# Scan operands with three PSUM banks instead of a rotation through four, decays in one piece in every scan, and a norm's first pieces issued inside a tick

## The chip, the cores and the metric

The kernel runs on one core of a Trainium2 chip, as one launch. A core has five engines with a queue of instructions each, which they work off in order: TensorE (PE in the profile, its weight loads PEld), VectorE (DVE), ScalarE (ACT), GpSimd (POOL) and SyncE (SP, which only starts DMAs here). Semaphores make one engine wait for another. The matmul results lie in PSUM, 8 banks of 128 x 512 float32. The metric is the device time of one execution in microseconds (us), as the median of several runs.

## The reference

Four blocks are added to an image x of shape (4, 128, 64, 64), one after the other; each first normalises its input over groups of channels (`_gn`). The third one, a state space scan, fills most of the time:

```python
x = x + attention(_gn(x))              # 1x1 q, k, v; softmax over the 4096 pixels
x = x + conv5x5(_gn(x))                # weights built from tables
t = einsum('oc,bchw->bohw', Wx, _gn(x)) + bx        # third block, per image
xF, xR = t[:, :64], flip(t[:, 64:])    # 64 channels forwards, 64 backwards
  xc = silu(conv1d(u, conv_w, 4 taps) + conv_b)
  delta = softplus(xc @ Wd + bd)
  Bm, Cm = xc @ WB, xc @ WC            # 64 states
  h[t] = exp(delta * A) * h[t-1] + (delta * xc) * Bm     # for 64 x 64 rows, 4096 steps
  y = sum_n h * Cm + D * xc
x = x + Wp @ concat(yF, flip(yR)) + bp
x = x + conv3x3(_gn(x)) + main_b       # offsets are computed in the reference and not used
```

## The kernel before, in words

All is float32. `program` (L1667) builds the work; the order of instructions on every engine is that in which the Python code issues them.

**The scan.** `scan_core` (L1426) goes through 1024 ticks, 256 an image: 4 chunks of 1024 pixels, 2 directions, 16 groups of 4 states, 2 groups of 32 channels; a tick handles 128 rows (32 channels x 4 states) of 1024 pixels. Its steps, each issued some ticks from the others in the loop over `i` (L1628):
- `drive(i + 2)`, L1535, GpSimd: `db = dx * br`. Both are read back from DRAM with replication, `dx` (delta * xc) and `de` (delta) by `steps`, `br` and `cr` (rows of Bm and Cm) by `row`. There are three buffers of `db`.
- `decay(i + 1)`, L1528, ScalarE: `da = exp(a * de)` into PSUM.
- `recur(i)`, L1545, VectorE: the scan instruction. It reads `da` and `db`, and takes `before`, the last column of the chunk ahead. Either its result goes to `hc` and GpSimd multiplies it with `cr` a tick later (`weigh`, L1566), or it goes back to `da` and VectorE multiplies (L1548) into `hc`. `to_pool` (L1448) chooses.
- `collect(i - 3)`, L1584, TensorE: sums `hc` over the states, into the bank "y".

**What lies beside it.** `images()` is a generator with all other work: attention, 5x5 convolution (`conv_pairs`) and scan operands of the next image, then the ends and 3x3 convolutions of earlier images. After each half tick the loop adds `pace / 2` of credit (`PACES`, L47: 2.60 in the first image's scan, 2.57 in the second and third, 1.55 in the last), and pulls pieces of that work until their announced costs use it up. A cost is what the generator yields: 0.86 for a product, 1.7 for a `HOP`, 0.7 for a `SLOT`.

**The operands.** `scan_prep` (L1237) settles the norm's sums (`settle`, L359: a few small VectorE steps, a small matmul, then two small GpSimd steps, which wait for the next tick by `next_tick`), and normalises the image in 8 pieces (L424, ScalarE). Ahead of six of them it waits while "wide" is there. `scan_operands` (L1262) then writes a list of slots. A chunk of 512 pixels, `i`, has slots from 5i on: taps (L1284, TensorE: four taps, forwards and backwards, into the bank `pt`), `halves` (L1299 and L1306, ScalarE: half of the sum, and tanh), `silu` (L1310, VectorE), three products (L1319) into the bank `pz` (for delta) and twice into "a" (the rows, which L1325 copies out), `softplus` (L1333, L1334), `exp` (L1362, L1368), `digits` (L1339, L1340, VectorE). `logs` (L1375) come in blocks of several chunks, since they load another table on ScalarE; after them `join` (L1347), the store of `dd`, `drives` (L1352, GpSimd) and its store `dxd`. Each slot yields 0.7. For the first image the operands of the first two chunks are made before tick 0; for the others all of them lie in the last ticks of the scan of the image before.

**The banks.** "s", "z", "a" and "y" are there always. The other four have two uses. Outside the operand stages they hold two decays of 1024 columns (pool "wide"). In a stage `widen` (L1805) closes this pool between two ticks and opens another one: "s2", one bank for the operands, and three of 512 columns for decays in halves; a scan is then two scans of 512. `pt` and `pz` go through "s", "z" and "s2" in turn. The two kinds of tick are told apart in `decay` and `recur` by `"wide" in pools`.

Of the kernel before, what the change touches and what calls it, by code (L numbers as in the profile page):

```python
# [32 lines left out]
P = 128  # L33
# [12 lines left out]
PRODUCT, VALUES, HOP, SLOT, AHEAD, EARLY = 0.86, 0.9, 1.7, 0.7, 4, 8  # L46
PACES = 2.60, 2.57, 2.57, 1.55  # L47
# [6 lines left out]
def conv_preact_kernel(  # L54
# [275 lines left out]
    class Sums:  # L330
# [28 lines left out]
        def settle(self, name, wait=False):  # L359
# [14 lines left out]
            if wait:  # L374
                yield from next_tick()
            nc.gpsimd.tensor_tensor(rs, var, mhalf, ALU.pow)
            nc.gpsimd.tensor_tensor(nb, minus, rs, ALU.mult)
            return rs, nb

# [72 lines left out]
    def attention_start(b, xn):  # L452
# [19 lines left out]
        def keys(i):  # L472

            tag = "saz"[i % 3] if b == 0 else "s" if i < 3 or i % 2 == 0 else "s2" if "s2" in pools else "z"
            pvs[i] = bank(tag, f"pv_{b}_{i}").rearrange("p (t c) -> p t c", c=C)
            for t in range(TPM):
                nc.tensor.matmul(
                    pvs[i][:, t, :], xn[:, bass.ts(i * TPM + t, P)], wv, start=True, stop=True
                )
# [547 lines left out]
    def conv_pairs(b, xs, tag, st, st2, lean):  # L1027
# [207 lines left out]
        ready.update({(b, "convolved"), "narrow"})  # L1235
# [4 lines left out]
    def scan_prep(b, xs, st, mats4):  # L1240
# [4 lines left out]
        gn = yield from st.settle(f"s{b}", True)  # L1245
        xn = pools["big"].tile([P, VSIZE], F32, tag="V", name=f"xn2_{b}")
        nc.gpsimd.memset(xn[:, :pad], 0.0)
        nc.gpsimd.memset(xn[:, pad + L : 2 * pad + L], 0.0)

        def piece(*chunks):  # L1250
            for i in chunks:
                cut = slice(i * MM, (i + 1) * MM)
                normalise(xn[:, pad + cut.start : pad + cut.stop], xs[:, cut], gn)
# [3 lines left out]
        piece(0)  # L1257
        piece(NM - 1)
        while "wide" in pools:
            yield HOP  # L1260
        return scan_operands(b, xn, mats4, piece)

    def scan_operands(b, xn, mats4, piece):
# [10 lines left out]
        def taps(i, *ks):  # L1274
            if ks[0] == 0:
                pts[i] = bank(ring["pt", i], f"pt_{b}_{i}")
# [65 lines left out]
        def join(c):  # L1342
            for i in range(c * CH // MM, (c + 1) * CH // MM):
                cut = bass.ts(i, MM)

                eng = nc.vector if b > 0 and NM // 2 <= i < NM - 1 else nc.gpsimd
# [8 lines left out]
        def delta_product(i):  # L1355
            pzs[i] = product(i, 0, ring["pz", i])
# [13 lines left out]
        def logs(i, j):  # L1370
            for n in range(i, j):
                to = us[n]
                if b > 0 and j == NM and n - i < 3:
                    to = bank(("a", "z", "s2")[n - i], f"ln_{b}_{n}")
# [5 lines left out]
        order = sorted([(EVERY * i, "pt", i) for i in range(NM)] + [(EVERY * i + 8, "pz", i) for i in range(NM)])  # L1380
        ring = {(what, i): ("s", "z", "s2")[n % 3] for n, (_, what, i) in enumerate(order)}
        ring["pz", NM - 1] = "z"
# [5 lines left out]
        for i in range(NM):  # L1388
# [3 lines left out]
            at(t + 4, halves, i)  # L1392
            at(t + 5, silu, i)
            at(t + 8, delta_product, i)
            at(t + 9, row_product, i, 1)
            at(t + 10, softplus, i)
            at(t + 11, row, i, 1)
            at(t + 12, exp, i)
            at(t + 12, row_product, i, 2)
            at(t + 13, digits, i)  # L1400
            at(t + 13, row, i, 2)
# [3 lines left out]
        for i, j in zip(cuts, cuts[1:]):  # L1405
            t = EVERY * (j - 1) + 15
            at(t, logs, i, j)
            for n, c in enumerate(range(i // PER, j // PER)):
                at(t + 1 + n, join, c)
                at(t + 3 + n, drives, c)  # L1410
                at(t + 4 + n, ready.add, (b, "operands", c))
# [5 lines left out]
        at(EVERY * (NM - 1) + 13, ready.add, "drives")  # L1417
        ready.add("operands")
        for t in range(max(slots) + 1):
            for f, args in slots.get(t, ()):  # L1420
                f(*args)
            yield SLOT
        ready.discard("operands")
        ready.discard("drives")
        ready.discard("narrow")
# [5 lines left out]
    def scan_core(mats4, ynds, before, widen, result):  # L1431
# [16 lines left out]
        def to_pool(i):  # L1448


            if i not in pooled:
                n = i % 5
                pooled[i] = (
                    i % 3 == 2 if "wide" in pools
                    else n == 1 if "drives" in ready
                    else n % 2 == 0 if "operands" in ready else n % 2 == 1
# [60 lines left out]
        def decay(i, h):  # L1517
            b, c, d, q, g = ticks[i]
            if h == 0:
                das[i] = []  # L1520
            elif "wide" in pools:
                return

            wide = "wide" in pools
            size = CH if wide else MM
            da = in_turn(*(("wide", "da", 2) if wide else ("s2", "half", 3)), [P, size], f"da_{i}_{h}")
            das[i].append(da)
            nc.scalar.activation(  # L1528
                da, rep["de", b, c, d, g][:, bass.ts(h, size)], AF.Exp, scale=a_neg[:, at(i)]
# [7 lines left out]
        def recur(i):  # L1537
# [3 lines left out]
            size = CH // len(das[i])  # L1541
            for n, da in enumerate(das.pop(i)):
                cut = bass.ts(n, size)
                h = hc[:, cut] if to_pool(i) else da
                nc.vector.tensor_tensor_scan(h, da, db[:, cut], before, ALU.mult, ALU.add)  # L1545
                before = h[:, size - 1 : size]
                if not to_pool(i):
                    nc.vector.tensor_tensor(  # L1548
                        hc[:, cut], h, rows["c", b, c, d, q][:, cut], ALU.mult
                    )  # L1550
            hcs[i], hold[i] = hc, before
# [78 lines left out]
        for i in range(-AHEAD, n + 4):  # L1630
# [5 lines left out]
            late = i + 1 < n and i >= 0 and widen()  # L1636
            if not late:
                do(decay, i + 1, 0)
            do(recur, i)
            if late:  # L1640
                do(keep, i)
                late()
                do(decay, i + 1, 0)
# [6 lines left out]
            do(decay, i + 1, 1)  # L1650
# [19 lines left out]
    def program(safe):  # L1670
# [3 lines left out]
        ready.add("narrow")  # L1674
# [120 lines left out]
        with ExitStack() as es, tc.manual_schedule():  # L1795
# [3 lines left out]
            banks = es.enter_context(ExitStack())  # L1799
# [155 lines left out]
```

## Time and profile before

| what | value |
|---|---|
| median of 3 runs | 4184.01 us (4183.44 to 4185.94) |
| the profiled execution, its own time | 4187.43 us |
| its span, first to last instruction | 4184.1 us |
| busy share: TensorE, VectorE, ScalarE, GpSimd | 88%, 84%, 56%, 84% |
| decays of 1024 columns, of 512 | 963, 122 |
| mean of such a decay | 1117 ns, 697 ns |
| before the first scan | 685.3 us |
| ticks | 685.3 to 4118.4 us |

The profile has a page of totals for the execution and, from the same trace, other views: busy time of each engine in given stretches, the instructions in order of time, groups of equal instructions, and sums of waits. In a line of instructions, `out<-in` are tiles by name, then come shapes; in brackets stands how long the engine was idle before it, and what released it. An instruction's duration overlaps the start of the next one by up to 0.1 us, so costs in a row are better taken from one start to the next.

### The profile page before, as it was taken

How to read it: one execution, taken by the hardware profiler on the slowest of the kernel's cores; microseconds unless marked ns; L12 is line 12 of the kernel's file. 1: busy time of each engine (PE TensorE's matmuls, PEld its weight loads, DVE VectorE, ACT ScalarE, POOL GpSimd, SP SyncE). 2: the span in 40 equal slices, each digit the busy share in tenths (PEclk: the TensorE clock that was granted, in tenths of full speed). 3: DMA queues.
4: the chain of work that ended last, by engine and by line, in shares of the span. 5: the costliest groups of instructions: out<-in, count | busy, mean ns of one | idle time of the engine just before them, and what ended most of it. 6: DMA issues, size and time to landing. Idle time of an engine off the chain costs nothing. (4 is left out here: it accounts for less than half of the span.)

```text
span 4184.1 us, 49830 instructions
## 1 busy us (share of the span) xinstructions
PE 3687.0 (88%) x17668; PEld 2140.8 (51%) x17668; DVE 3514.0 (84%) x2441; ACT 2325.1 (56%) x3900; POOL 3525.7 (84%) x1688
## 2 busy tenths in 40 slices
PE   8999997999999979999999889999998576675856
PEld 4444443778875327887763368787733121221212
DVE  3842215999999979999999899999998899999996
ACT  3344306667665476766664676666645654545442
POOL 2433315999999979999999799999998899999995
PEclk9999998999999989999999999999999788797877
DMA  1020006555555666555555575555655756666661
GB/s 66 31 104 26 3 11 239 196 191 191 195 190 190 192 240 222 197 192 194 192 190 193 203 253 195 191 197 185 204 179 197 258 199 230 205 213 224 211 234 61
DMA packets 223728, 740.99 MB, mean 177 GB/s; under 512 B 29662, under 2 KB 30942, under 8 KB 223212
## 3 DMA queue, kind: packets, MB, share of 16 engines
q1 hardware_dynamic: 221548, 736.99, 52.0%
q8 instruction: 140, 2.29, 0.2%
q14 instruction: 120, 0.98, 0.1%
q10 hardware_dynamic: 1920, 0.73, 0.1%
HBM read 662.14 MB, written 75.47 MB: 176 GB/s over the span
## 5 line engine op out<-in xcount | busy, mean ns | idle before, releaser
L1535 POOL TENSOR_TENSOR db<-dx,br 128x1024 f32<-128x1024 f32 x1024 | 2398.5, 2367 | 119.4 <-DVE hc L1545 44.6
L1528 ACT ACTIVATE da<-de,a_neg 128x1024 f32<-128x1024 f32 (+1 forms) x1085 | 1160.3, 1070 | 375.2 <-DVE hc L1548 272.6
L1545 DVE TENSOR_TENSOR_SCAN da<-da,last,db 128x1024 f32<-128x1024 f32 (+1 forms) x500 | 1152.8, 2306 | 21.7 <-ACT last L1561 10.6
L1548 DVE TENSOR_TENSOR hc<-da,cr 128x1024 f32<-128x1024 f32 (+1 forms) x698 | 824.7, 1182 | 61.8 <-issue 1.3
L1566 POOL TENSOR_TENSOR hc<-hc,cr 128x1024 f32<-128x1024 f32 x354 | 837.4, 2366 | 6.8 <-ACT last L1561 3.6
L1584 PE MATMUL y<-hc,sel 128*32 128x512 f32 x4096 | 601.3, 649 | 270.2 <-POOL hc L1566 206.9
L748 PEld LDWEIGHTS acc<-v,exchange 128*128 128x128 f32 x6144 | 799.7, 191 | 48.3 <-issue 10.6
L727 PE MATMUL sc<-r,x 128*128 128x256 f32 x3072 | 803.0, 386 | 21.2 <-ACT exchange L740 16.2
L748 PE MATMUL acc<-v,exchange 128*128 128x129 f32 x6144 | 803.3, 275 | 1.5 <-ACT exchange L740 1.5
L727 PEld LDWEIGHTS sc<-r,x 128*128 128x128 f32 x3072 | 527.9, 191 | 188.5 <-ACT exchange L740 41.2
L1545 DVE TENSOR_TENSOR_SCAN hc<-da,last,db 128x1024 f32<-128x1024 f32 (+1 forms) x268 | 597.3, 2229 | 7.0 <-ACT last L1561 3.6
L740 ACT ACTIVATE exchange<-sc 128x512 f32<-128x512 f32 x768 | 441.8, 588 | 171.9 <-PE sc L727 164.6
L1584 PEld LDWEIGHTS y<-hc,sel 128*32 128x32 f32 x4096 | 113.6, 113 | 620.6 <-POOL hc L1566 303.4
L1545 DVE TENSOR_TENSOR_SCAN da<-da,db 128x1024 f32<-128x1024 f32 (+1 forms) x170 | 376.6, 2215 | 14.9 <-ACT da L1528 10.5
L1561 ACT COPY last<-da 128x1 f32<-128x1 f32 x511 | 80.4, 157 | 542.9 <-DVE hc L1548 541.9
L549 POOL TENSOR_TENSOR sidep<-sidep,exchange 128x512 f32<-128x512 f32 x120 | 165.0, 1375 | 254.3 <-ACT exchange L531 251.9
L531 ACT ACTIVATE exchange<-sc 128x512 f32<-128x512 f32 x256 | 152.6, 596 | 254.5 <-PE sc L530 246.5
L549 DVE TENSOR_TENSOR sided<-sided,exchange 128x512 f32<-128x512 f32 x120 | 98.5, 821 | 214.7 <-ACT exchange L531 213.6
L537 PE MATMUL acc<-exchange,v 128*128 128x512 f32 x512 | 261.9, 594 | 0.9
L530 PE MATMUL sc<-r,x 128*128 128x512 f32 x512 | 262.1, 594 | 0.6 <-ACT r L513 0.6
L893 PE MATMUL pcm<-xpm,cs 128*128 128x512 f32 x432 | 213.0, 643 | 10.3 <-ACT xpm L424 10.3
L1545 DVE TENSOR_TENSOR_SCAN hc<-da,db 128x1024 f32<-128x1024 f32 (+1 forms) x86 | 190.7, 2218 | 7.6 <-ACT da L1528 5.1
(295 smaller groups left out, 3048.6 us busy)
## 6 DMA issues: line engine op xcount, KB each, us to landing
br<-bm SPq DMA_DIRECT2D x512, 512.0 KB, 4.0
cr<-cm SPq DMA_DIRECT2D x512, 512.0 KB, 4.6
dx<-dxd SPq DMA_DIRECT2D x64, 512.0 KB, 5.3
de<-dd SPq DMA_DIRECT2D x64, 512.0 KB, 6.3
xs<-in_x_dram SPq DMA_DIRECT2D x16, 512.0 KB, 6.0
xsd<-xs SPq DMA_DIRECT2D x16, 512.0 KB, 5.2
xcd<-xc SPq DMA_DIRECT2D x16, 512.0 KB, 2.6
bm<-bs SPq DMA_DIRECT2D x32, 256.0 KB, 5.4
```

Of the source, the lines that this page charges most:

```text
L530: nc.tensor.matmul(sc, xn[:, bass.ts(j, P)], rq[blk], start=True, stop=True)
L537: nc.tensor.matmul(acc[blk], v[:, j, :C], ring[:, u % NRING, :], start=j == 0, stop=j == NJT - 1)
L549: eng.tensor_tensor(s, s, ring[:, u % NRING, :], ALU.add)
L727: nc.tensor.matmul(sc[:, bass.ts(n, HM)], xn[:, bass.ts(2 * k + n, P)], rq[blk][:, cut], start=True, stop=True,)
L740: nc.scalar.activation(pt, sc, AF.Exp)
L748: nc.tensor.matmul(acc[part][:, bass.ts(t, CV)], ring[:, u % NRING, n * HM + t * P : n * HM + (t + 1) * P], v[:, 2 * k + n, :], start=(k, ...
L1528: nc.scalar.activation(da, rep["de", b, c, d, g][:, bass.ts(h, size)], AF.Exp, scale=a_neg[:, at(i)])
L1535: nc.gpsimd.tensor_tensor(dbs[i], rep["dx", b, c, d, g], rows["b", b, c, d, q], ALU.mult)
L1545: nc.vector.tensor_tensor_scan(h, da, db[:, cut], before, ALU.mult, ALU.add)
L1548: nc.vector.tensor_tensor(hc[:, cut], h, rows["c", b, c, d, q][:, cut], ALU.mult)
L1566: nc.gpsimd.tensor_tensor(hcs[i], hcs[i], rows["c", b, c, d, q], ALU.mult)
L1584: nc.tensor.matmul(y[r : r + SG, :], sel, hcs[first + gg][:, bass.ts(h, MM)], start=False, stop=q == NQ - 1, tile_position=(0, r), skip_gr ...
```

## The change

- The pool "wide" is opened once, ahead of the ticks, and stays. `widen`, "s2" in the scans, and the halves of decays and scans are gone; each decay has 1024 columns, and each scan is one instruction.
- The operands use three banks in a fixed way: `pt` "s", `pz` "z", the rows "a". The last logs of an image go to two banks, not three, and one `join` less is on VectorE. `keys` of the next image take "s" while operands are made.
- The slots of a chunk are moved: halves from 4 to 3, silu from 5 to 4, the delta product from 8 to 6, softplus from 10 to 7, and so on; digits from 13 to 10. Logs stand at 11 after the last chunk's first slot and not at 15. A slot yields `STEP` = 0.9 as long as chunks are in work; the slots behind that wait for the next tick. `PACES` are 2.66, 2.60, 2.60 and 1.57.
- `settle` leaves its GpSimd steps and the norm's pieces 0 and 7 to a hook. The loop over ticks runs it just ahead of the next decay.
- `to_pool`: while operands are made, ticks with i mod 5 of 2 or 4 are weighed on GpSimd (before: 0, 2, 4), while the last products are made those of 1 (as before), otherwise each third (before, in the stretches with "s2" and no operands: 1 and 3 of 5).

```diff
-PRODUCT, VALUES, HOP, SLOT, AHEAD, EARLY = 0.86, 0.9, 1.7, 0.7, 4, 8
-PACES = 2.60, 2.57, 2.57, 1.55
+PRODUCT, VALUES, HOP, SLOT, STEP, AHEAD, EARLY = 0.86, 0.9, 1.7, 0.7, 0.9, 4, 8
+PACES = 2.66, 2.60, 2.60, 1.57
...
-            if wait:
-                yield from next_tick()
-            nc.gpsimd.tensor_tensor(rs, var, mhalf, ALU.pow)
-            nc.gpsimd.tensor_tensor(nb, minus, rs, ALU.mult)
+            def finish():
+                nc.gpsimd.tensor_tensor(rs, var, mhalf, ALU.pow)
+                nc.gpsimd.tensor_tensor(nb, minus, rs, ALU.mult)
+                if then:
+                    then((rs, nb))
+            if then:
+                hooks.append(finish)
+                while hooks and ticks_begun[0]:
+                    yield 0.4
+                run_hooks()
+            else:
+                finish()
...
-        piece(0)
-        piece(NM - 1)
-        while "wide" in pools:
-            yield HOP
+        def first(gn):
+            scale_shift.append(gn)
+            nc.gpsimd.memset(xn[:, :pad], 0.0)
+            nc.gpsimd.memset(xn[:, pad + L : 2 * pad + L], 0.0)
+            piece(0)
+            piece(NM - 1)
+        yield from st.settle(f"s{b}", first)
...
-                pts[i] = bank(ring["pt", i], f"pt_{b}_{i}")
+                pts[i] = bank("s", f"pt_{b}_{i}")
...
-                eng = nc.vector if b > 0 and NM // 2 <= i < NM - 1 else nc.gpsimd
+                eng = nc.vector if b > 0 and NM // 2 <= i < NM - 2 else nc.gpsimd
...
-            pzs[i] = product(i, 0, ring["pz", i])
+            pzs[i] = product(i, 0, "z")
...
-                if b > 0 and j == NM and n - i < 3:
-                    to = bank(("a", "z", "s2")[n - i], f"ln_{b}_{n}")
+                if b > 0 and j == NM and n - i < 2:
+                    to = bank("az"[n - i], f"ln_{b}_{n}")
...
-            at(t + 4, halves, i)
-            at(t + 5, silu, i)
-            at(t + 8, delta_product, i)
-            at(t + 9, row_product, i, 1)
-            at(t + 10, softplus, i)
-            at(t + 11, row, i, 1)
-            at(t + 12, exp, i)
-            at(t + 12, row_product, i, 2)
-            at(t + 13, digits, i)
-            at(t + 13, row, i, 2)
+            at(t + 3, halves, i)
+            at(t + 4, silu, i)
+            at(t + 6, delta_product, i)
+            at(t + 7, softplus, i)
+            at(t + 7, row_product, i, 1)
+            at(t + 8, row, i, 1)
+            at(t + 9, exp, i)
+            at(t + 9, row_product, i, 2)
+            at(t + 10, digits, i)
+            at(t + 10, row, i, 2)
...
-            t = EVERY * (j - 1) + 15
+            t = EVERY * (j - 1) + 11
...
-            yield SLOT
+            if t <= EVERY * (NM - 1) + 10:
+                yield STEP
+            else:
+                yield from next_tick()
...
-                    i % 3 == 2 if "wide" in pools
-                    else n == 1 if "drives" in ready
-                    else n % 2 == 0 if "operands" in ready else n % 2 == 1
+                    n == 1 if "drives" in ready
+                    else n % 2 == 0 and n > 0 if "operands" in ready else i % 3 == 2
...
+            das[i] = in_turn("wide", "da", 2, [P, CH], f"da_{i}")
...
-            late = i + 1 < n and i >= 0 and widen()
-            if not late:
-                do(decay, i + 1, 0)
+            run_hooks()
+            do(decay, i + 1)
```

## The prediction

> **What bounds the kernel now.** I read the page first, then the busy time by stretch, with the stretches cut at the starts of scans (a scan on VectorE is one tick's; counting them numbers the ticks), then the timelines of the operand stages. A tick is one scan step of the loop; 1024 of them fill 685 to 4118 us.
>
> ```profile
> PE 3687.0 (88%) x17668; PEld 2140.8 (51%) x17668; DVE 3514.0 (84%) x2441; ACT 2325.1 (56%) x3900; POOL 3525.7 (84%) x1688
> ...
> L1535 POOL TENSOR_TENSOR db<-dx,br 128x1024 f32<-128x1024 f32 x1024 | 2398.5, 2367 | 119.4 <-DVE hc L1545 44.6
> L1528 ACT ACTIVATE da<-de,a_neg 128x1024 f32<-128x1024 f32 (+1 forms) x1085 | 1160.3, 1070 | 375.2 <-DVE hc L1548 272.6
> ```
> GpSimd makes each tick's drive `db`, VectorE the scan, ScalarE the decay `da`. 1085 decays are 1024 ticks with 61 in two halves.
>
> ```profile
> core 0: us, PE busy (x) PEld busy (x) DVE busy (x) ACT busy (x) POOL busy (x), PEclk, DMA share, GB/s
> ...
> 750.40:1246.90 496.50, 491.29 (x3371) 398.09 (x3371) 478.97 (x276) 341.52 (x622) 485.49 (x210) 1.00 0.58 192
> ...
> 1453.40:1604.30 150.90, 120.66 (x542) 56.54 (x544) 118.23 (x114) 103.69 (x169) 124.04 (x61) 0.90 0.68 237
> ...
> 2320.30:2472.90 152.60, 122.65 (x571) 62.73 (x571) 124.25 (x116) 108.18 (x177) 130.97 (x64) 0.89 0.68 242
> ...
> 3411.00:4118.40 707.40, 463.32 (x1456) 138.77 (x1448) 686.93 (x383) 335.85 (x522) 690.37 (x310) 0.79 0.63 212
> ```
> Rows one and four are plain ticks (156 in 496.5 us, 224 in 707.4): 3.18 and 3.16 us a tick, VectorE and GpSimd at 96 to 98%. In the first, beside attention, TensorE is at 99% too. Rows two and three hold an operand stage, 32 and 34 ticks at 4.7 and 4.5 us, and no engine is above 86%. At 3.16 us a tick they hold 50 and 45 us too much; the third such stage (3187 to 3358, 38 ticks) 50.5. Only there and in the first image's operands (before tick 0) does the change move instructions.
>
> What is lost in the first such stage, on VectorE and on ScalarE:
>
> ```profile
> 1488.70 1.28 DVE L1545 TENSOR_TENSOR_SCAN hc<-da,hc,db 128x512 f32<-128x512 f32 x1 [3.48 <-ACT da L1528]
> ...
> 1535.04 0.70 DVE L1339 SCALAR_TENSOR_TENSOR pb<-u,pb 128x512 f32<-128x512 f32 x1 [6.20 <-ACT u L1368]
> ...
> 1569.17 1.88 DVE L1347 TENSOR_TENSOR exchange<-exchange,ln 128x512 f32<-128x512 f32 x3 [7.13 <-ACT ln L1375]
> ```
> ```profile
> 1566.01 0.69 ACT L1528 ACTIVATE da<-de,a_neg 128x512 f32<-128x512 f32 x1 [6.11 <-DMA de<-dd]
> ```
> The second half of a decay stands behind norm pieces (3.48); digits wait for `u` behind the logs (6.20); and at the end a decay waits for the DMA of the new image's `de`, the last logs stand behind it, and VectorE idles 7.13 us for them. From scan 241 (1479.4) to scan 260 (1585.1) are 105.7 us for 19 ticks, 45.7 above 60.0. The same 19 ticks take 102.4 in the second stage, 109.7 in the third; of the latter 8.2 are the final weights at L917 to L920, which later fall behind the stretch: 101.5.
>
> **The change, part by part.**
>
> Whole decays. 61 ticks lose a half. By starts in the timeline a half decay costs ScalarE 0.62 and a whole one 1.05: 0.19 saved a tick. VectorE spends 3.86 us on a halved tick that it weighs itself (scan 1.32, product 0.61, twice) and 3.52 on a whole one; 2.50 and 2.26 where GpSimd weighs: 28 x 0.34 + 33 x 0.24 = 17 us, 6 a stage. Fewer weighings go to GpSimd (2 of 5, not 3 of 5).
>
> Slots. A chunk still takes 5 slots, but a slot costs 0.9, not 0.7, and paces are 2.66 and 2.60 instead of 2.60 and 2.57: 1.7 ticks a chunk instead of 1.35. So the stage covers more ticks, and each extra tick hides 3.16 us.
>
> Three banks. `pt` has only "s", `pz` only "z". A chunk's cycle becomes a loop, counted from the end of its tanh on ScalarE: exp and identity of the chunk before, 1.2; its two digits on VectorE, 1.3, free "z"; the product, 1.0; the other half of the next taps, 1.8; the row product, 1.0; its copy, 0.5; two halves, 1.15. With waits of 0.1 that is 8.1 us, and 9.7 where a whole scan of 2.3 stands between silu and digits. (Durations are spacings of starts in the timelines: an activation of 512 is 0.57, exp 0.62, a copy 0.48, a step of digits 0.63, 16 tap matmuls 3.6, a product 0.95.) Following the four queues in order through the first stage, from scan 237 at 0, tanh ends at 9.9, 17.3, 26.4, 36.2, 44.3, 55.6 (logs between), 65.4 and 73.5. One cycle in full: tanh 3 ends at 36.2, exp and identity of chunk 2 at 37.4, its digits at 38.8, product 3 at 39.8, the other taps at 41.6, the row product at 42.6, its copy at 43.1, halves and tanh 4 at 44.3; beside it ScalarE makes a decay and VectorE a scan. Before, tanh starts are 1491.2, 1496.6, 1503.6, 1510.7, 1519.1, 1525.3, 1536.6, 1544.7: 53.5 us for seven cycles against 63.6. But 63.6 cover 12.1 ticks, 53.5 only 9.6; above 3.16 a tick that is 25 against 23. The middle loses 2.
>
> Beginning. Pieces 0 and 7 go before the decay: the settled mean at 0, pow and product 0.95, pieces 1.4, decay done at 3.45, when VectorE ends scan and product of its tick (3.52): no wait. GpSimd is idle for it (its next drive needs the scan before). The six other pieces (4.3) still hold the next decay, and silu(0) waits some 3 us. Before, VectorE lost 0.89 + 3.48 + 1.88 + 0.88. Without that cover the pair costs 1.4 us a stage. Gain: 2.
>
> End. The first logs stand at tick 245, ten ticks ahead of the new image, no longer six, so the `de` load (issue to landing 6.3 us) is there. From the last tanh, VectorE reaches scan 256 at 96.0: 22.5 us for 5 ticks, 6.5 above; before, 39.8 for 7.8 ticks, 15.2 above. Gain: 9. The last logs have two banks, no longer three, which moves one join of 512 (0.63) from VectorE to GpSimd (1.24), which has room there. The last four slots now wait a tick each; what stands behind them, the next attention, is late by nothing, since the last drive product stands ahead of tick 260's drive before and of 259's now.
>
> Stage one then takes 96.0 for its 19 ticks, not 105.7. Walking the second likewise gives 98.0 (a y group of 1.85 stands between taps and product), the third some 95.5 (no next image on ScalarE): gains 9.7, 4.4, 6.0, together **20**. Bounds: summing in each tick the largest of ScalarE's, VectorE's and GpSimd's work gives 158, 165 and 181 before (measured 151, 153, 171) and 152, 162 and 178 after: only 11 gained. If all waits went, an excess of 16.6 would stay in each (half of the 17.6 us that operands add on VectorE and the 15.6 on GpSimd), 50 of 129.6: 79 gained.
>
> First image. No scan hides its loop: 7.5 us a chunk against some 6.9, but operands of the first chunk are made in 20 slots, not 24, so tick 0 follows u(4), at 676.7, and not the next chunk's relu, abs and row (685.35). Work left then costs ticks 0 to 16 about 62.5 instead of 65.1. Gain **11**; bounds: 0, where the longer loop takes it, and 14.
>
> Paces. TensorE is at 99% beside attention. At 2.60 those ticks took 3.18, at 2.57 (503.1 for 160, 494.2 for 156) 3.15 and 3.17. By that slope 2.66 costs 0.03 a tick over 153, and 2.60 in two images 0.02 over 317, up to 12; nothing if TensorE's 1% holds it. I take **6** lost. SP's queue gets the same transfers; xsd stores move with their pieces, ahead of the operands.
>
> The Trainium skill speaks against it. TensorE waits little for a bank before: "PE pb L1319 <- ACT bs L1325" is 30.9 us in 16 waits, all on "a". Its page Perfetto Trace Analysis, Optimizing Tensor Performance, Matmuls, says independent matmul groups should rotate through banks, so that one's evacuation lies beside the next one's matmuls. If every evacuation lay bare (halves 1.15 and digits 1.3, in 24 chunks), 58 us would be lost and the median would be 4184 + 58 = 4242; by the loop above most of that is in the 8.1 us already, and longer ticks cover it.
>
> Sum: 20 + 11 - 6 = 25. The profiled execution took 4187.4 (span 4184.1), 3.4 above the median 4184.0. 4187.4 - 25 = 4162.4, in the median **4159**. The operand loop is the number I trust least.
>
> **Rivals.**
> 1. Only paces and split change, loop as long as its ticks: gain 0 to 8, 4176 to 4184. For: the sum of maxima gives 11 and paces take 6 to 12. Against: the 6.1 and 7.1 waits do go.
> 2. Slower: the loop through the single "z". Digits stand on VectorE behind scan and product; each whole scan and product of VectorE's (3.52) that comes between more than I have put there lengthens the cycle. My walk has 8.7 us on average without logs; with 25 / 24 = 1.05 us more in each of 24 chunks the gain is gone, and with such a scan and product in every second chunk, 1.76 us on average, 42 are lost: 4201. For: in these ticks the three engines have nearly equal work. Against: ScalarE has two decay buffers and so one tick of room.
> 3. Better: stages lose most waits, gain 45 to 79 there, 4105 to 4139. For: no engine is above 86%. Against: the loop.
> 4. Attention ticks become TensorE's: 12 instead of 6, 4165; within the forecast.
>
> **Numbers.** Forecast (gain of 10 to 44): 0.50, 4140 to 4175. Rival 3: 0.10. Rival 1: 0.18. Rival 2: 0.22. 0.2% is 8.4 us, about what a measurement of this kernel tells from no change. Faster 0.60, same 0.18, slower 0.22. Since both signs hold much, the range reaches from 4130 into rival 2, 4200.
>
> **What would show it.** Right: all decays 128x1024; tick 0 near 677; scans 237 to 256 in 96; tanh starts 8 to 10 apart; no `de` wait near 256; plain ticks beside attention at 3.16 to 3.21. Wrong: tanh starts over 10 apart, with L1337's product waiting for VectorE; attention ticks above 3.22; a `de` or `dx` wait at a new image.

## The result, and the profile after

The changed kernel takes 4200.29 us (median of 6 runs, 4197.99 to 4202.84), the kernel before 4184.98 in the same comparison: ratio 1.0034, 95% interval 1.0022 to 1.0047. It is slower, by some 14 us (0.34%); a gain of 25 was forecast. The profiled execution took 4200.1 us (span 4198.1).

The page after, with the lines that answer to those of before:

```profile
PE 3688.2 (88%) x17668; PEld 2128.0 (51%) x17668; DVE 3514.7 (84%) x2360; ACT 2318.2 (55%) x3839; POOL 3506.8 (84%) x1680
...
L1543 POOL TENSOR_TENSOR db<-dx,br 128x1024 f32<-128x1024 f32 x1024 | 2400.5, 2368 | 153.3 <-DVE hc L1551 63.7
L1536 ACT ACTIVATE da<-de,a_neg 128x1024 f32<-128x1024 f32 x1024 | 1144.3, 1118 | 327.9 <-DVE hc L1553 253.0
```

Decays are whole now, 1024 of one form. VectorE has the same work to 0.7 us, ScalarE and GpSimd have less; the added time is idle time. GpSimd's ahead of `db` went from 119.4 to 153.3 us. The same busy time by stretch, cut at the same scans (16, 172, 234, 266, 490, 524, 800, 1024):

```profile
core 0: us, PE busy (x) PEld busy (x) DVE busy (x) ACT busy (x) POOL busy (x), PEclk, DMA share, GB/s
...
747.90:1244.60 496.70, 496.05 (x3422) 404.38 (x3421) 478.99 (x276) 345.89 (x627) 484.44 (x209) 1.00 0.59 192
1452.40:1602.70 150.30, 121.73 (x542) 57.75 (x541) 118.40 (x89) 101.64 (x152) 117.75 (x59) 0.91 0.69 240
2321.70:2479.80 158.10, 118.57 (x560) 56.45 (x559) 122.20 (x90) 105.42 (x158) 124.15 (x62) 0.94 0.66 233
...
3424.40:4129.90 705.50, 461.82 (x1457) 138.19 (x1455) 686.75 (x383) 335.63 (x522) 690.87 (x310) 0.78 0.63 213
```

The ticks beside attention take 496.7 us, not 496.5: nothing lost there. The first stage takes 150.3, not 150.9, with VectorE's work the same and GpSimd's 6 us less; the second 158.1, not 152.6; the third (scans 746 to 784) 179.5, not 170.6. Tick 0 comes at 681.3 (685.3 before), scan 16 at 747.9 (750.4).

To see where in a stage the time is, I cut each in three, at its first and at its last tanh, and take from each part 3.16 us for every scan begun in it. What remains is the excess; one part is good to a tick, their sum does not depend on the cuts. In us, for the three stages:

| kernel | to the first tanh | first to last tanh | to the end | sum |
|---|---|---|---|---|
| before | 12.5 + 12.2 + 11.6 | 21.9 + 24.7 + 27.1 | 15.3 + 8.2 + 11.9 | 145 |
| after | 8.8 + 8.7 + 9.0 | 29.0 + 35.9 + 39.8 | 11.3 + 6.0 + 10.6 | 159 |

So the beginning gained 10, the end 7.5, and the middle, the eight chunks themselves, lost 31. From scans 237, 492 and 748, each one tick ahead of the scan in which its stage's first tanh falls, 19 ticks take 100.4, 104.3 and 106.9 us; 96.0, 98.0 and 95.5 were forecast. Tanh starts are now 9.6, 10.5 and 11.1 us apart on average in the three stages; before they were 7.6, 8.0 and 7.9 apart.

One long cycle of the second stage, from the timelines of ScalarE, VectorE and TensorE of the changed kernel (start, duration, then the idle time in brackets):

```profile
2361.39 0.66 ACT L1324 ACTIVATE pt<-pt,hbias 128x512 f32<-128x512 f32 x1
2361.96 0.58 ACT L1380 ACTIVATE pb<-pb 128x512 f32<-128x512 f32 x1
2362.58 0.69 ACT L1386 ACTIVATE u<-pb,ones 128x512 f32<-128x512 f32 x1
...
2372.34 0.59 ACT L1343 COPY bs<-pb 128x512 f32<-128x512 f32 x1 [3.54 <-PE pb L1337]
2372.82 0.69 ACT L1317 ACTIVATE xc<-pt,hbias 128x512 f32<-128x512 f32 x1
2373.41 0.66 ACT L1324 ACTIVATE pt<-pt,hbias 128x512 f32<-128x512 f32 x1
```
```profile
2362.70 2.34 DVE L1551 TENSOR_TENSOR_SCAN hc<-da,last,db 128x1024 f32<-128x1024 f32 x1
2364.95 0.67 DVE L1357 SCALAR_TENSOR_TENSOR pb<-u,pb 128x512 f32<-128x512 f32 x1
2365.66 0.69 DVE L1358 TENSOR_TENSOR exchange<-exchange,pb 128x512 f32<-128x512 f32 x1
...
2374.10 0.69 DVE L1328 SCALAR_TENSOR_TENSOR xc<-pt,xc 128x512 f32<-128x512 f32 x1 [4.23 <-PE pb L1337]
```
```profile
2366.40 1.12 PE L1337 MATMUL pb<-xc,bdiag 128*128 128x512 f32 x2 [1.62 <-DVE exchange L1358]
2367.46 1.94 PE L1302 MATMUL pt<-xn,wtap 128*64 128x512 f32 x8
2369.32 1.92 PE L1587 MATMUL y<-hc,sel 128*32 128x512 f32 x16
2371.18 1.13 PE L1337 MATMUL pb<-xc,bdiag 128*128 128x512 f32 x2
```

Read it round: `u` is there at 2363.2, but the digits stand on VectorE behind a scan until 2364.95. They free "z" at 2366.3. Only then come the delta product, the other half of the taps, a y group and the row product. ScalarE has waited 3.54 us for that row, copies it, and only then makes halves and tanh, 12 us after the last tanh. VectorE in turn stands 4.23 us at silu, which is put down to TensorE although tanh releases it, and the scans behind it stand too.

At the first stage's end something else stands. VectorE, then ScalarE, of the changed kernel:

```profile
1573.41 2.30 DVE L1551 TENSOR_TENSOR_SCAN da<-da,db 128x1024 f32<-128x1024 f32 x1 [1.98 <-ACT da L1536]
...
1578.13 2.30 DVE L1551 TENSOR_TENSOR_SCAN da<-da,db 128x1024 f32<-128x1024 f32 x1 [1.11 <-ACT da L1536]
```
```profile
1568.86 0.59 ACT L498 COPY v<-pv 128x512 f32<-128x512 f32 x1 [1.15 <-PE pv L493]
1571.61 0.59 ACT L498 COPY v<-pv 128x512 f32<-128x512 f32 x1 [2.17 <-PE pv L493]
1572.09 0.19 ACT L1564 COPY last<-hc 128x1 f32<-128x1 f32 x1
1572.18 1.12 ACT L1536 ACTIVATE da<-de,a_neg 128x1024 f32<-128x1024 f32 x1
```

The `de` wait of this stage is gone, as forecast (the third stage has one now, 3.75 us at tick 769). In its place the next attention's `v` copies and products take turns, 2.75 us each, since the keys have only "s" until the slots are over; decays stand behind copies that wait.

### The profile page after: what moved, and what is told of

Its sections match the earlier page's. It is cut to its first block, busy times and chain, and to the rows that moved or that the text cites. A ratio compares the mean times of both kernels' runs of the same rounds, so it can differ in the third digit from the quotient of the medians.

```text
span 4198.1 us, 49596 instructions
## 1 busy us (share of the span) xinstructions
PE 3688.2 (88%) x17668; PEld 2128.0 (51%) x17668; DVE 3514.7 (84%) x2360; ACT 2318.2 (55%) x3839; POOL 3506.8 (84%) x1680
## 5 line engine op out<-in xcount | busy, mean ns | idle before, releaser
L1543 POOL TENSOR_TENSOR db<-dx,br 128x1024 f32<-128x1024 f32 x1024 | 2400.5, 2368 | 153.3 <-DVE hc L1551 63.7
L1536 ACT ACTIVATE da<-de,a_neg 128x1024 f32<-128x1024 f32 x1024 | 1144.3, 1118 | 327.9 <-DVE hc L1553 253.0
L1551 DVE TENSOR_TENSOR_SCAN da<-da,last,db 128x1024 f32<-128x1024 f32 x509 | 1192.2, 2342 | 26.3 <-POOL db L1543 9.8
L1553 DVE TENSOR_TENSOR hc<-da,cr 128x1024 f32<-128x1024 f32 x681 | 833.8, 1224 | 59.7 <-DVE da L1551 0.5
L1569 POOL TENSOR_TENSOR hc<-hc,cr 128x1024 f32<-128x1024 f32 x343 | 811.8, 2367 | 8.4 <-ACT last L1564 5.9
L743 PE MATMUL sc<-r,x 128*128 128x256 f32 x3072 | 800.1, 385 | 11.6 <-ACT exchange L756 4.5
L1551 DVE TENSOR_TENSOR_SCAN hc<-da,last,db 128x1024 f32<-128x1024 f32 x259 | 606.1, 2340 | 2.2 <-ACT da L1536 1.3
L1551 DVE TENSOR_TENSOR_SCAN da<-da,db 128x1024 f32<-128x1024 f32 x172 | 392.7, 2283 | 22.8 <-ACT da L1536 15.7
L1551 DVE TENSOR_TENSOR_SCAN hc<-da,db 128x1024 f32<-128x1024 f32 x84 | 191.5, 2280 | 3.8 <-ACT da L1536 3.8
```

The lines of the kernel that those rows point to most:

```text
L743: nc.tensor.matmul(sc[:, bass.ts(n, HM)], xn[:, bass.ts(2 * k + n, P)], rq[blk][:, cut], start=True, stop=True,)
L1536: nc.scalar.activation(das[i], rep["de", b, c, d, g], AF.Exp, scale=a_neg[:, at(i)])
L1543: nc.gpsimd.tensor_tensor(dbs[i], rep["dx", b, c, d, g], rows["b", b, c, d, q], ALU.mult)
L1551: nc.vector.tensor_tensor_scan(h, da, db, before, ALU.mult, ALU.add)
L1553: nc.vector.tensor_tensor(hc, h, rows["c", b, c, d, q], ALU.mult)
L1569: nc.gpsimd.tensor_tensor(hcs[i], hcs[i], rows["c", b, c, d, q], ALU.mult)
```

## The experiments

Theory A: the loop through the banks is what costs; "z" is held until VectorE has come to the digits, "s" until it has come to silu, and everything behind stands in order. Rivals: B, the stage's end (keys on "s"); C, the slots and the ticks in a chunk set the cycle, whatever the banks. Sums of excess are in the table at the end of this part.

**1 to 3. Tanh and exp to SBUF.** For tanh:
```diff
-            ths[i] = pt if b > 0 else pools["bg"].tile(
-                [P, MM], F32, tag="w", bufs=4, name=f"th_{b}_{i}"
-            )
+            ths[i] = pools["bg"].tile([P, MM], F32, tag="w", bufs=4, name=f"th_{b}_{i}")
```
For exp:
```diff
-            nc.scalar.activation(pzs[i], pzs[i], AF.Exp, scale=-1.0)
+            pz = pzs[i]
+            pzs[i] = pools["bg"].tile([P, MM], F32, tag="w", bufs=4, name=f"ex_{b}_{i}")
+            nc.scalar.activation(pzs[i], pz, AF.Exp, scale=-1.0)
```


> The tanh of the second to fourth image's operands goes to a tile in SBUF and no longer in place over the taps' bank "s"; nothing else changes. Theory A (the loop: "s" and "z" are held until VectorE has come round to silu and to digits): the taps then wait for ScalarE's tanh only; the waits of L1302 for silu (3.9, 8.4 and 8.4 us in the three stages of the changed kernel) go, cycles from tanh to tanh fall from about 10.4 to 9.5 us, and the kernel gains 8 to 20 us: 4180 to 4192. Theory B (the stage's end: keys of the next image all on "s", decays behind their copies): nothing at 2 us or more, 4200. Theory C (the slots: 1.7 ticks a chunk set the cycle): nothing, 4200.

> The exp of the delta product goes to a tile in SBUF and no longer in place over the bank "z", so that the next delta product waits for ScalarE's exp and not for VectorE's digits. Theory A: the waits of L1337 for digits (6.0, 9.6 and 11.7 us in the three stages) go, and with them part of ScalarE's waits for the product (12.4, 16.6, 19.2); gain 8 to 20 us, 4180 to 4192. Theory B: 4200. Theory C: 4200. Against a gain under A: the same four small tiles then hold the row copies and the exp, so a copy may wait for its store.

> Both at once: tanh and exp to SBUF, so neither operand bank is held by VectorE. Theory A: the loop is short, tanh starts are 8 to 9 us apart, the three stages fall by 20 to 40 us together: 4160 to 4180, below the kernel before. Theory B: 4200, tanh starts closer but the end later by as much. Theory C: 4200, and tanh starts stay 10 apart.

Measured: 4211.39 (1.0064, interval 1.0050 to 1.0078), 4211.55 (1.0061, 1.0047 to 1.0074), 4210.60 (1.0058, 1.0045 to 1.0072). All three theories missed; the kernels are slower than the changed one. The banks did come free, each alone: with tanh in SBUF TensorE's wait for silu goes, but its wait for digits on "z" grows from 27.4 to 44.8 us over the three stages, and the stages are 10.5 us longer. With exp in SBUF the wait for digits goes, the one for silu on "s" grows from 20.7 to 32.7, and many cycles are 8.5 us. The three stages take as long as in the changed kernel (0.3 us more), and 10.7 of the profiled execution's 11.5 us lie in ticks 0 to 16 (77.2 us, not 66.6), since the edit moves the first image's exp too. There the first image's digits take 21.6 us of VectorE and not 11.0. In the stages VectorE pays too, and what the free bank gives there beside that is not separated. VectorE and GpSimd of the kernel with exp in SBUF:

```profile
1505.91 0.67 DVE L1357 SCALAR_TENSOR_TENSOR ex<-u,ex 128x512 f32<-128x512 f32 x1
1506.61 2.72 DVE L1358 TENSOR_TENSOR exchange<-exchange,ex 128x512 f32<-128x512 f32 x1
1509.25 2.35 DVE L1553 TENSOR_TENSOR_SCAN da<-da,last,db 128x1024 f32<-128x1024 f32 x1
```
```profile
1506.07 2.72 POOL L1545 TENSOR_TENSOR db<-dx,br 128x1024 f32<-128x1024 f32 x1 [3.06 <-DVE hc L1553]
1508.74 2.80 POOL L1571 TENSOR_TENSOR hc<-hc,cr 128x1024 f32<-128x1024 f32 x1
```

The second step of the digits, 0.69 us in each of the 32 cases of the changed kernel, where one operand is in PSUM, took 2.7 us in 13 of 32 here, where both are in SBUF. It started inside a GpSimd instruction and ended 0.5 us after that one's end, as if it had begun there. Summed, silu and digits cost VectorE 70 us in the changed kernel, 80 with tanh in SBUF, 118 with exp (40 of the 48 more in the stages) and 142 with both. So these runs do not tell A from C: they take a wait away and put a stall in. Why tanh alone loses 11 us, with only 10 of stall and the wait moved to the other bank, I have not followed further.

**4. Keys on two banks.**
```diff
-            tag = "saz"[i % 3] if b == 0 else "s" if i % 2 == 0 or "operands" in ready else "z"
+            tag = "saz"[i % 3] if b == 0 else "s" if i % 2 == 0 or ("operands" in ready and "joined" not in ready) else "z"
...
+        at(EVERY * (NM - 1) + 12, ready.add, "joined")
```


> Keys of the next image take "s" and "z" in turn as soon as the last digits and joins are issued, and not "s" alone until the stage is over. Theory B: the copy-and-product chain of 2.75 us each at the stage's end halves, decays no longer stand behind copies that wait for TensorE (7.1 and 4.3 us), scans 256 to 260 of the first two stages take 14 us and not 18.6; gain 5 to 10, 4190 to 4195. Theory A: at most 3 us, 4197 to 4200. Theory C: 4200.

4196.23 (1.0028, 1.0017 to 1.0038). In the first stage the end's excess falls from 11.3 to 5.3, and scans 234 to 266 from 150.2 to 144.2, as B says. The second and third stage give 2.6 and 3.8 back. B is real in the first stage; in all it is worth some 4 us of 14, and the two intervals overlap.

**5. "z" and "a" swapped from chunk to chunk.** This frees the delta product from the digits without SBUF.
```diff
-            pzs[i] = product(i, 0, "z")
+            pzs[i] = product(i, 0, "za"[i % 2])
...
-            pbs[i, m] = product(i, m, "a")
+            pbs[i, m] = product(i, m, "az"[i % 2])
```


> Of the changed kernel, the delta product takes "z" and "a" in turn from chunk to chunk, and the rows the other one; nothing goes to SBUF. Then the next delta product waits for a row copy on ScalarE and not for digits on VectorE. Theory A (the loop over the banks): the waits of TensorE for digits (27 us in the three stages) go or halve, tanh starts come closer than 10.4 us on average, gain 10 to 20: 4180 to 4190. Theory B (the end, keys on "s"): 4200. Theory C (the cycle is set by its ticks): waits move to ScalarE's decays and VectorE's scans; within 3 of 4200.

4184.02 (0.9993, 0.9984 to 1.0002): the whole loss is gone, with nothing moved but the banks. TensorE's waits from the first stage to the end of the third, first of the changed kernel, then of this one (total, times, longest):

```profile
PE pb L1337 <- DVE exchange L1358: 27.4, 17, 2.9
PE pt L1302 <- DVE xc L1328: 20.7, 20, 3.2
```
```profile
PE pt L1302 <- DVE xc L1328: 19.7, 20, 3.2
...
PE pb L1337 <- DVE exchange L1358: 1.7, 1, 1.7
```

The wait for digits falls from 27.4 to 1.7 us, the one for silu on "s" stays. The middle's excess goes from 105 to 84. This is A.

**6. The first row product one slot earlier.**
```diff
-            at(t + 7, row_product, i, 1)
+            at(t + 6, row_product, i, 1)
```


> Of the changed kernel, the first row product is issued one slot earlier: on TensorE right behind the delta product and ahead of the other half of the next chunk's taps. Its copy on ScalarE, behind which halves and tanh stand, then no longer ends the loop. Theory A: a product and a copy with their hand-overs (some 1 us a chunk) come off the cycle of 24 chunks, less the 1 us by which the taps come later: gain 5 to 20, 4180 to 4195. Theory B: 4200. Theory C: 4200.

4193.31 (1.0018, 1.0009 to 1.0027): 7 us below the changed kernel, within A's 5 to 20. The row's copy no longer ends the loop. Waits for digits stay (25.5), and the third stage keeps cycles of 12.4.

**7. All three.** Swap, earlier row product, keys.

> The swap of "z" and "a", the earlier row product and the keys on "s" and "z" in turn, all three in one kernel. Theory A: loop and end both shorter, 20 to 35 less than the changed kernel: 4165 to 4180, below the kernel before. Theory B: as keys alone, 4196. Theory C: 4196.

4169.42 (0.9961, 0.9948 to 0.9975), faster than both kernels, as A has it. One cycle on TensorE, in the second stage:

```profile
2338.11 1.94 PE L1302 MATMUL pt<-xn,wtap 128*64 128x512 f32 x8 [1.01 <-DVE xc L1328]
2340.10 2.10 PE L1337 MATMUL pb<-xc,bdiag 128*128 128x512 f32 x4
2342.13 1.94 PE L1302 MATMUL pt<-xn,wtap 128*64 128x512 f32 x8
```

Delta and row product stand together, in this cycle with no wait for digits; tanh starts are 8.7, 9.1 and 9.6 us apart. Of TensorE's waits in a chunk the one for silu is the longest left: 23.3 us in the three stages, beside 8.1 for row copies and 6.9 for digits.

**8. The single banks alone, in the kernel before.**
```diff
-        ring = {(what, i): ("s", "z", "s2")[n % 3] for n, (_, what, i) in enumerate(order)}
+        ring = {(what, i): "s" if what == "pt" else "z" for _, what, i in order}
```


> The kernel before with one part of the change: taps always in "s", delta products always in "z"; "s2" is left for a logs' output only, decays stay in halves, slots and costs as before. Theory A: the single banks alone cost 10 to 30 us, 4195 to 4215, and tanh starts go from 7.9 us apart to 9 or more. Theories B and C: within 4 of the kernel before, 4181 to 4189.

4209.78 (1.0056, 1.0042 to 1.0070): 23 us, nearly all in the middle (74 to 96 of excess). Tanh starts are 8.9, 9.1 and 8.9 us apart, just short of the 9 named. TensorE now has the two waits of A, which the kernel before does not have in these stages:

```profile
PE pt L1284 <- DVE xc L1310: 19.7, 15, 2.5
...
PE pb L1319 <- DVE exchange L1340: 10.5, 7, 3.6
```

A again, without any other part of the change. Here the wait for silu on "s" is the longer one, so how the 23 us divide between "s" and "z" stays open.

**9 and 10. Slots, and paces, of the kernel before, in the changed kernel.**
```diff
-            at(t + 3, halves, i)
-            at(t + 4, silu, i)
+            at(t + 4, halves, i)
+            at(t + 5, silu, i)
...
-                yield STEP
+            yield SLOT
```


> The changed kernel with the slots of the kernel before: its places of halves, silu, products and digits, its logs at 15, 0.7 a slot to the end. Single banks, whole decays, paces and the norm's hook stay. Theory A: the single banks cost what they cost in the kernel before (23 us there), whole decays give some back: 4192 to 4210. Rival (the new places of the slots were what cost, not the banks): 4175 to 4188.

> The changed kernel with slots, costs and paces of the kernel before; of the change there stay single banks, whole decays, the hook and the choice of ticks weighed on GpSimd. Beside the kernel before with single banks alone (4210) it shows what whole decays and the hook are worth when the stage begins at the same tick. By the prediction's terms (halves cost VectorE 6 us a stage, the beginning 2): 10 to 24 below 4210, 4186 to 4200. If VectorE is not what the stage waits for: 4204 to 4212.

With slots alone 4217.86 (1.0070, 1.0057 to 1.0083), with slots and paces 4198.75 (1.0030, 1.0018 to 1.0043). The first began its stages in ticks 237, 489 and 741 (first tanh) and not in 242, 497 and 752; it lies 8 us above A's range and says little. The second does: beside experiment 8 whole decays with the hook are worth 11 us (with what else of the change stays in it: fewer ticks weighed on GpSimd, one `join` less on VectorE, and the keys on "s", which experiment 4 prices at some 4 us), and beside the changed kernel the new slots with their paces are worth nothing in the sum: tick 0 comes 8 us earlier with them (681.3, not 689.3), and the ticks behind it take that back. So, added in this order, the change is single banks +23, whole decays and hook -11, slots and paces +2, the last no more than noise.

**11. The old paces alone.**
```diff
-PACES = 2.66, 2.60, 2.60, 1.57
+PACES = 2.60, 2.57, 2.57, 1.55
```


> The changed kernel with the paces of the kernel before (2.60, 2.57, 2.57, 1.55), nothing else. The prediction's term: 6 us gained, bounds 0 to 12, 4188 to 4200. By the traces of before and after (3.182 and 3.184 us a tick beside attention): nothing in those ticks; what moves is where a stage begins among the ticks: 4196 to 4204.

4230.65 (1.0104, 1.0089 to 1.0119): 30 us slower, where the prediction's term has 6 gained. The ticks beside attention take 494.2 us, 2.5 less than with 2.66; the first two stages 159.5 and 172.3, some 23 more. The first stage begins in tick 244 (first tanh) and not 238, and is not done in time. VectorE there:

```profile
1537.80 0.69 DVE L1358 TENSOR_TENSOR exchange<-exchange,pb 128x512 f32<-128x512 f32 x1
1545.79 0.69 DVE L1328 SCALAR_TENSOR_TENSOR xc<-pt,xc 128x512 f32<-128x512 f32 x1 [7.31 <-ACT pt L1324]
1547.06 0.70 DVE L1357 SCALAR_TENSOR_TENSOR pb<-u,pb 128x512 f32<-128x512 f32 x1 [0.58 <-ACT u L1386]
1547.79 0.69 DVE L1358 TENSOR_TENSOR exchange<-exchange,pb 128x512 f32<-128x512 f32 x1
1548.40 2.34 DVE L1551 TENSOR_TENSOR_SCAN hc<-da,last,db 128x1024 f32<-128x1024 f32 x1
```

From 1534 to 1548 there is no scan. Four ticks ahead of a new image the program (`before`, L1833) pulls its work until the operands of the first chunk are made, with no tick between. From scan 251, 507 and 763 to the next are 17.8, 22.1 and 24.9 us here, 3.5, 2.3 and 4.8 in the changed kernel. These gaps are 54 us longer in all, the three stretches around them only 26 (9, 14 and 2), presumably since what is made in a gap need not be made behind it; another 6.5 lie in ticks 0 to 16. So paces set the tick at which a stage stands, and the trace bears out reading D below for paces that are too low.

**12. Higher paces** (2.72, 2.64, 2.64).

> The changed kernel with paces of 2.72, 2.64, 2.64 and 1.57. Reading D (paces set at which tick a stage begins; with 2.60 and 2.57 it began at tick 244 and its last chunks were pulled through with few ticks before the new image, 30 us): the stage begins some 5 ticks earlier than at 2.66, nothing is pulled through there already, so 4195 to 4203. Reading E (the paces' term of the prediction, TensorE's ticks beside attention): as much again as from 2.60 to 2.66, up to 12 slower, 4205 to 4215; attention ticks above 3.2. Reading F (the 30 us were chance of how waits fell): anywhere by 20 either way.

4242.90 (1.0133, 1.0118 to 1.0149), worse than any reading had it. The attention ticks of the first image (scans 16 to 172) now take 507.0 us, 3.25 each, with TensorE busy for 505.4 of it: E, and it starts between 2.66 and 2.70 (505.7 there, in experiments 13 to 16). A stage too early is no gain: scan 251 is followed at 5.1 us (3.5 with 2.66). Over the three images these ticks cost some 21 us; the other 22, most of them around the second stage, I have not followed, and F is not excluded for those. Lower and higher both lose with these slots.

**13 to 16. Ticks in a chunk,** by the cost of a slot: 0.7, 1.0 and 1.1 in the kernel of experiment 7; 1.1 and 1.3 there with higher paces; 1.1 with higher paces in the changed kernel.

> The kernel with swap, row product and keys (4169), with a slot at 0.7 and not 0.9, so 1.3 ticks a chunk and not 1.7. Theory A (the loop has its length whatever ticks lie in it): each chunk hides 0.4 ticks less, 10 us a stage, of which the cycles give a part back by a scan less; slower by 5 to 20, 4174 to 4190. Theory C (ticks set the cycle): cycles shorten by as much as ticks leave, 4165 to 4172.

> The kernel with swap, row product and keys, with a slot of 1.0 and the paces of the change. Between its 0.9 (4169) and its 1.1 (4162): 4158 to 4168 if the ticks hidden in the loop decide; lower, 4152 to 4158, if 1.1 already came late at the end of the third stage.

> The same kernel with a slot at 1.1, so 2.1 ticks a chunk. Theory A: each chunk hides 0.4 ticks more; cycles stay at 8 to 10 and the stages lose 5 to 10 us each, 4140 to 4160, unless operands come too late for the new image's first ticks (then a wait for its loads near ticks 256, 512 and 768 takes 5 to 15 of it back). Theory C: the cycle grows by the added ticks, 4166 to 4172.

> The kernel with swap, row product, keys and a slot of 1.1 (4162), with paces of 2.70, 2.64, 2.64 and 1.57, so that the stages of 2.1 ticks a chunk begin earlier. Reading D: its third stage ended beyond tick 768 (last tanh in tick 769); earlier, the last chunks come with their ticks, 5 to 15 gained: 4147 to 4158. Reading E: 5 to 10 lost, 4167 to 4172.

> The same with a slot of 1.3 (2.4 ticks a chunk) and paces of 2.74, 2.68, 2.68 and 1.57. Theory A: another 0.4 ticks a chunk are hidden in the loop as long as a cycle (8 to 10 us) is longer than its ticks' own work on VectorE (2.4 x 3 + 2 = 9.2): little is left, 0 to 10 below the run with 1.1; above it only if the stage's end comes late again. 4140 to 4160.

> The changed kernel, with neither swap nor row product nor keys, with a slot of 1.1 and paces of 2.70, 2.64, 2.64 and 1.57. Theory A: the loop through the single "z" is as long as before (10.4) but holds 2.1 ticks (6.6 us of a free tick's time) and not 1.7; of the 31 us that the three edits of the loop and the end gave, a half comes back this way: 4180 to 4192. If each tick added lengthens the loop by a scan and product (3.5): 4196 to 4204.

Measured, with the ratio to before and its interval:

| slot, paces | us | ratio |
|---|---|---|
| 0.7 | 4216.41 | 1.0073 (1.0061 to 1.0086) |
| 0.9 (experiment 7) | 4169.42 | 0.9961 (0.9948 to 0.9975) |
| 1.0 | 4187.58 | 1.0002 (0.9993 to 1.0011) |
| 1.1 | 4162.49 | 0.9943 (0.9932 to 0.9955) |
| 1.1, 2.70 and 2.64 | 4183.40 | 0.9995 (0.9986 to 1.0004) |
| 1.3, 2.74 and 2.68 | 4202.14 | 1.0045 (1.0031 to 1.0059) |
| changed kernel, 1.1, 2.70 and 2.64 | 4218.15 | 1.0081 (1.0067 to 1.0095) |

The best is 4162.49, 24 us below the kernel before and 38 below the changed one. Fewer ticks (0.7) lose, as A says, but 47 us and not 5 to 20: the middle's excess is 109 and not 78, tick 0 comes 10 us later (691.5), and stages begin too early (first tanh of the third in tick 740), which I have not priced. More ticks (1.1) gain, though 2 us less than A's range: the middle's excess goes from 78 to 68, although operands are late now in two stages (15.8 and 18.2 us from scans 507 and 763 to the next, 2.3 and 4.8 with 0.9). The run with 1.0 missed: it should lie between its neighbours and doesn't. Its first two stages are 9 and 8 us longer than with 0.9, and the second has cycles of 13.1 and 12.5. (Its attention ticks of the first image take 500.7 us against 496.3, but with 1.1 they do too.) Which of a chunk's steps a scan falls behind is decided anew by each setting, and these sizes are not predicted by A. Higher paces remove that (2.3 and 4.8 again with 2.70), but the attention ticks become longer: 19 of the 21 us by which that run is slower than the same slots with 2.66, and above both readings. With 1.3, 42 us above A's range, it is the same: the middle's excess falls to 57, and the attention ticks take 35 us longer than in the best run. In the changed kernel (last row) the three stretches around the stages together are 7 us shorter, and the attention ticks 20 longer: neither of my two numbers for it.

Excess of the three stages, added up, for the kernels on which the reading rests ("the same, whole decays, hook" is the second kernel of 9 and 10):

| kernel | to first tanh | first to last | to the end | sum | median |
|---|---|---|---|---|---|
| before | 36 | 74 | 35 | 145 | 4184 to 4188 |
| before, single banks | 37 | 96 | 33 | 166 | 4210 |
| the same, whole decays, hook | 30 | 97 | 31 | 159 | 4199 |
| after | 27 | 105 | 28 | 159 | 4200 |
| after, swap | 27 | 84 | 28 | 140 | 4184 |
| after, swap, row, keys | 27 | 78 | 22 | 127 | 4169 |
| the same, slot of 1.1 | 28 | 68 | 25 | 122 | 4162 |

## Why the prediction was wrong, point by point

- *"The middle loses 2"*: this step failed. It lost 31 in the three stages. The loop itself was the right one: in the first stage tanh ends at 9.9, 18.4, 27.9, 38.1, 46.6, 58.0, 68.2 and 76.8, against 9.9, 17.3, 26.4, 36.2, 44.3, 55.6, 65.4 and 73.5 forecast. It was 0.5 us a cycle too short, in hand-overs that I had at 0.1 in all: in the cycle that ends at 1511.3 us each step's result comes 0.05 to 0.2 us later than the spacing of starts that I added. That "s" is held until silu, since tanh is written back into it, I had missed; it costs TensorE 20.7 us of waits, and what it costs in the end no run shows, since the one that took it away went to SBUF. The second and third stage are worse, 73.8 and 77.7 us for seven cycles; in the long cycle shown above a y group and a scan fell inside the loop. I had the third as the quickest, since no next image is on ScalarE; it was the slowest.
- *"longer ticks cover it"*, the step that set the cost aside, failed with it. 12 free ticks are worth 38 us, 10 are worth 32; that paid 6 of the 13 to 22 us by which the seven cycles became longer.
- *"End. Gain: 9"*, and *"what stands behind late by nothing"*: in the first two stages `de` and logs are in time, as said, but keys on one bank put `v` copies ahead of decays. The first stage's end gained 4 and not 9, the three together 7.5; experiment 4 shows that keys on two banks bring 6 more in the first.
- *"Beginning. Gain: 2"*: 3 to 4 a stage, 10 in all. Right, and small.
- *Whole decays, 6 us a stage on VectorE*: with the hook they are worth 11 us (experiment 8 and the second kernel of 9 and 10), 7 of it in the beginnings, where the decay behind norm pieces stood. In the middle they bring nothing (96 and 97): what VectorE saves there it waits.
- *"First image. Gain 11"*: 4 at tick 0, 2.5 at tick 16. The same loop: tanh starts are 8.5 us a chunk apart and not 7.5 (7.3 before). The bound of 0 was the nearer one.
- *"Paces. I take 6 lost"*: nothing is lost in the attention ticks (3.184 for 3.182), and taken back alone they cost 30. I had priced a pace by the ticks that it fills and not by the tick at which the stage then begins. The slope that I feared is there, only above 2.66 (505.7 us for those ticks with 2.70, 507.0 with 2.72).
- *Rival 2, 4201*: the mechanism and, by chance of its assumed 1.76 us a chunk, the price. What would show it (tanh starts over 10 apart, L1337 waiting for VectorE) is what the trace shows. Measured were 1.3 us a cycle above the walk, over 21 cycles. I gave it 0.22 because the walk stood against it; but the walk shows its steps for the first stage only, and the other two, where it has 98.0 and 95.5, took 104.3 and 106.9.
- The page Perfetto Trace Analysis of the Trainium skill (Optimizing Tensor Performance, Matmuls) wants groups rotated through banks. The runs agree: giving the rotation up costs 23 us by itself, and a swap of two banks brings 16 of it back. The estimate made from its rule, 58 us, was too high.
- Small slips in the sums: 24 x (1.15 + 1.3) is 59 and not 58; the sums of maxima fall by 6 + 3 + 3 = 12 and not 11; 503.1 us for 160 ticks are 3.14 and not 3.15 a tick. None moves the forecast by more than 1 us.

## What to carry over

Ask of each buffer which engine's instruction gives it back, and what stands ahead of that instruction in its queue: a bank given back by an engine that has 2.3 us scans in its queue is held for the scan too, and here two buffers that change places from one piece to the next took most of that out (27.4 to 1.7 us) without moving anything else. That no engine is busy throughout says nothing in such a loop; follow one cycle round all its queues, in every stage and not in the easiest one. Where background work is metered against a foreground loop, its rate also sets where each later stage stands, so rate and stage have to be set together.

## What the runs showed of the hardware that was not expected

VectorE and GpSimd stop each other in one case. Silu and digits with one operand in PSUM took 0.69 us whatever GpSimd did: 48 of them began inside one of its products in the changed kernel, and none was longer. With both operands in SBUF, 32 steps of the digits began inside such a product in the kernel with exp in SBUF; they took 0.76 to 2.8 us, and one 7.5 as three more products came in a row, and each ended 0.55 us after a product's end. The GpSimd product beside them took 2.72 and 2.80 in the lines above and not 2.36. The page SBUF — State Buffer of the Trainium skill (SBUF: two separate sides) says that a VectorE step with two SBUF inputs and a GpSimd step that reads SBUF take turns on a shared pair of ports, whole instructions at a time; experiments 1 to 3 agree. Here this made PSUM the cheaper place for what VectorE reads beside a busy GpSimd: freeing "z" by exp in SBUF gained nothing in the stages, where silu and digits took 40 us more, and swapping two banks gained 16.
